# Four graph layers on one core: two layers' biases written into PSUM by ScalarE instead of added to x by GpSimd

## The chip, the core and the metric

The kernel runs on one core of a Trainium2 chip. A core has five engines with queues of their own: TensorE (PE; the loading of its weights is shown apart, as PEld), VectorE (DVE), ScalarE (ACT), GpSimd (POOL) and SyncE (SP), which here issues all DMAs. Matrix products go into PSUM, eight banks of 128 partitions x 512 fp32 elements; everything else lives in SBUF. The metric is the device time of one execution in microseconds (us), lower is better. The time before is the median of three runs, 1694.06 us (1693.2 to 1696.14).

## What is computed

32 graphs of 512 nodes with 128 features go through four residual layers, all with the same 512 x 512 adjacency of zeros and ones. Each layer normalises x over its features, takes the positive part, h, and adds the layer's result to x. In the reference, cut to what matters:

```python
# layer 0: attention-like weights from node scores
x_h = elu(h @ Wi + bi)
e = sigmoid(a_tgt[:, :, None] + a_src[:, None, :] + be[0]) * mask
recv = elu(concat([e @ x_h, x_h * sum(e)]) @ Wn + bn)
x = x + (concat([recv, x_h]) @ Wm + bm)
# layer 1: five gated steps
for _ in range(5):
    m = adj @ h; av = concat([m, m]); u3 = h @ u3_w.T + u3_b
    z, r = sigmoid(av @ w3_w.T + w3_b + u3), sigmoid(av @ w4_w.T + w4_b + u3)
    h = (1 - z) * h + z * tanh(av @ w5_w.T + w5_b + (r * h @ u5_w.T + u5_b))
x = x + h
# layer 2
x = x + (adj @ (h @ weight) + bias)
# layer 3: products with adj, adj^2, adj^3 and a weight for each
x = x + y
```

The change concerns `bm` of layer 0 and `bias` of layer 2, two vectors of 128 numbers that are the same for all nodes.

## The kernel before, in words

The kernel is written as a list of operations, which a planner orders. `op` (L55) takes an operation's engine, its assumed cost in us, a due time, the code that emits it, and the values that it reads and writes. `Plan.order` (L109) then plays the engines against each other in assumed time: each engine that is free takes the ready operation with the earliest due time, if a buffer is free for each value that it writes for the first time. What comes out is one order for each engine's queue, so any change of an operation's engine, cost or dependences makes all orders anew behind it. The planner keeps POOL's operations and DVE's operations that are marked `two` (two SBUF inputs) from overlapping in its assumed time (`shared`, L134 and L177).

A value (`Val`, L23) has a kind, and takes a buffer of that kind: "x" for a group of four graphs' x, "f" for [128, 512] SBUF tiles, "r" and "q" for rounded parts of such tiles, "s" for small statistics, "m" and "d" for DRAM scratch, and "b" for a PSUM bank. There are eight banks, and a graph's [512, 128] matrix fills one as four chunks of 128 columns (`chunks`, L277).

Graphs are staggered. The first four start 14 us apart; from then on a graph starts every 56 us and the last ones every 30, and a graph's four layers lie so far apart that layers of several graphs interleave on all engines. Layer 3 works on four graphs together, at the end of each group. What is done before the branch on the adjacency (whether it is exact in the rounded format; here it is) is ordered first; then each arm of the branch is ordered for itself, and the exact arm runs. There PE multiplies by the adjacency in rounded fp32 parts (low and high), and by weights in full fp32, which the trace shows as two records for each product.

The parts that the change touches, and that the prediction's steps name:

- `layernorm` (L448): DVE takes the moments (L457 to L460), POOL the power (L462), DVE the shift (L465), ACT four activations of one chunk each, from x to h (L470).
- `add_bias` (L436): one POOL operation for a graph that adds a broadcast [128, 128] bias tile to the graph's x in place (L437). It is called once for a graph in `first_layer` (L658, with `bm_bc`), after the layer norm has read x, and once in `layer2` (L857, with `l2b_bc`).
- `layer0` (L530): the product with Wi and an ELU (L519, L433, L522 on ACT, L524 and L526 on DVE), messages and node scores (L548, which writes two small pieces into each of two banks), the attention tiles (L599 on ACT, L602 on DVE), their sums on POOL (L621) and PE (L633, with L628 on DVE ahead of it), the products with them (L610), `own` on DVE (L636), the product with Wn, a second ELU, then the last product with the two halves of Wm into a bank `po` (L646): for each chunk two matmuls, of which the first starts the chunk anew (`start=n == 0`). `add_to_x` (L441) has DVE add the bank to x (L445).
- `layer1` (L807): products with u3T, w4T, w3T, w5T and u5T (all on L428), copies from PSUM by ACT (L417), gates on DVE (L824, L831) and ACT (L433), the new state on DVE (L841 to L845), and between steps a transpose through DVE (L369) and two DMAs, then the split into parts on ACT (L769) and DVE (L773). `times_adj` (L793) makes the adjacency products (L799).
- `layer2` (L857): parts, `times_adj`, a copy `m` from PSUM by ACT (L417), one matmul for each chunk with l2w into a bank `po` (L863), and DVE's addition to x (L445).
- `layer3` (L871): products L880 and L889 in one bank for four graphs, of which only the first starts anew; parts of it (L769, L773); DVE adds the end result to x (L901) and SP stores it (L906).

Of the kernel before, what the change touches and what calls it, by code (L numbers as in the profile page):

```python
# [28 lines left out]
        self.slot, self.writer, self.readers, self.left = None, None, [], 0  # L29


class Op:
    def __init__(self, eng, us, result, emit, two, keep):
        self.eng, self.us, self.result, self.emit, self.two, self.keep = eng, us, result, emit, two, keep
# [4 lines left out]
class Plan:  # L39
# [7 lines left out]
    def __init__(self, slots, ahead, last):  # L47
        self.ahead, self.last, self.ops, self.vals = ahead, last, [], {}
        self.free = {k: [(0.0, i) for i in range(n)] for k, n in slots.items()}
        self.until = dict.fromkeys(self.RESULT, 0.0)  # L50
        self.shared, self.now = 0.0, 0.0
        self.slack = 0.0
        self.idle = None

    def op(self, eng, us, due, emit, reads=(), writes=(), two=False, keep=0, result=None,  # L55
# [37 lines left out]
    def back_to(self, state):  # L93
# [5 lines left out]
            )  # L99
        self.free = {k: [*f] for k, f in free.items()}  # L100

    def known(self, o, to):

        own = {"PE": 0.0, "ACT": 0.13, "DVE": 0.13}
        if to.eng == o.eng in own:
            return o.known - o.result + own[o.eng]
        return o.known + (self.slack if to.eng == "PE" else 0.0)

    def order(self, end=None):  # L109

        left = [o for o in self.ops if not o.begun]
        for o in reversed(left):
            o.chain = o.us + max([0.0, *(o.result + a.chain for a in o.after)])
            if end is None:
                o.due = min(o.due, self.last - o.chain)
        by_due, oldest = sorted(left, key=lambda o: o.due), 0
        coming, ready = {e: [] for e in self.until}, {e: [] for e in self.until}
        order, events, index = [], [self.now], {}
        for i, o in enumerate(left):
            index[o] = i  # L120
            o.waits = sum(not b.begun for b in o.before)
            o.ready = max([o.earliest, *(self.known(b, o) for b in o.before if b.begun)])
            if not o.waits:
                heapq.heappush(coming[o.eng], (o.ready, i, o))
                events.append(o.ready)
        events += self.until.values()
        events += [t for f in self.free.values() for t, _ in f] + [self.shared]
        events = [max(t, self.now) for t in events]
        heapq.heapify(events)

        def begins(o, now):
            if o.due > by_due[oldest].due + self.ahead:
                return False
            if (o.two or o.eng == "POOL") and self.shared > now:  # L134
                return False
            keep = 0 if o is by_due[oldest] else o.keep
            return all(
                len(self.free[v.kind]) > keep and self.free[v.kind][keep][0] <= now
                for v in o.takes
            )  # L140

        while events:
            now = heapq.heappop(events)
            if end is not None and now >= end:
                break
            for e in self.until:
                while coming[e] and coming[e][0][0] <= now:
                    _, i, o = heapq.heappop(coming[e])
                    heapq.heappush(ready[e], (o.due, i, o))
                if self.until[e] > now:  # L150
                    continue
                passed, o = [], None
                while ready[e] and o is None:
                    x = heapq.heappop(ready[e])
                    if begins(x[2], now):
                        o = x[2]
                    else:
                        passed.append(x)
                for x in passed:
                    heapq.heappush(ready[e], x)  # L160
                if o is not None and end is not None and any(
                    c.due < o.due and t < now + 0.3 * o.us for t, _, c in coming[e]
                ):
                    heapq.heappush(ready[e], (o.due, index[o], o))
                    o = None
                if o is None and e == "PE" and end is not None and self.idle.known <= now:
                    order.append(self.idle)
                    self.until[e] = now + self.idle.us
                    heapq.heappush(events, self.until[e])
                if o is None:  # L170
                    continue
                order.append(o)
                o.begun = True
                while oldest + 1 < len(by_due) and by_due[oldest].begun:
                    oldest += 1
                o.start, self.until[e] = now, now + o.us
                if o.two or e == "POOL":  # L177
                    self.shared = self.until[e]
                for v in o.takes:
                    v.slot = self.free[v.kind].pop(0)[1]  # L180
                o.known = self.until[e] + o.result
                heapq.heappush(events, self.until[e])
                heapq.heappush(events, o.known)
                for v in o.vals:
                    v.left -= 1
                    if not v.left and v.kind:
                        self.free[v.kind].append((o.known, v.slot))
                        self.free[v.kind].sort()
                for a in o.after:
                    if a in index:  # L190
                        a.waits -= 1
                        a.ready = max(a.ready, self.known(o, a))
                        if not a.waits:
                            heapq.heappush(coming[a.eng], (a.ready, index[a], a))
        assert end is not None or len(order) == len(left), "the plan does not end: too few buffers"
        self.now = end or 0.0
        return order
# [3 lines left out]
def tile_four_graph_layers(  # L201
# [150 lines left out]
    def transposed(src, due):  # L352

        pt = Val("b")
        def emit():
            for c in range(NC):
                nc.tensor.transpose(at(pt)[:, ts(c, P)], at(src)[:, ts(c, P)], at(ident))
        op("PE", T_TR, due, emit, [src, ident], [pt])
        return pt
# [73 lines left out]
        op("ACT", us, due, lambda: nc.scalar.activation(  # L433
            at(dst), at(src), AF.Tanh, bias=at(bias), scale=scale), [src, bias], [dst])

    def add_bias(b, bias_bc, due):  # L436
        op("POOL", 1.4, due, lambda: nc.gpsimd.tensor_tensor(  # L437
            at(X[b]), at(X[b]), at(bias_bc)[:, None, :].to_broadcast([P, NC, D]), op=ALU.add),
            [X[b], bias_bc], [X[b]])

    def add_to_x(b, p, due, view=chunks, two=False):  # L441
        def add():
# [47 lines left out]
            [short, A_nat[ic]], [odd, n_odd], two=True)  # L490
    for jc in range(NC):
        pt, z = Val("b"), Val("f")
        def turn(jc=jc, pt=pt):
            for ic in range(NC):
                nc.tensor.transpose(at(pt)[:, ts(ic, P)], at(A_nat[ic])[:, ts(jc, P)], at(ident))
# [5 lines left out]
            at(mask)[:, jc, :], at(pt), 0.0, at(z), op0=ALU.is_equal, op1=ALU.add),  # L501
            [pt, z], [mask])
    p_odd = Val("b")
    def count():
        for jc in range(NC):
            nc.tensor.matmul(
# [23 lines left out]
    def layer0(b, h, due):  # L530
# [10 lines left out]
        msg, ends = Val("f"), Val("s")  # L541
        for half in range(2):
            pt = Val("b")
            def cut(pt):
                return at(pt)[:, : 2 * (P + 2)].rearrange("p (c d) -> p c d", c=2)
            def send(pt=pt, half=half):
# [41 lines left out]
                )  # L588
        if b < G:
            tgt = Val("b")  # L590
            op("PE", T_TR, d, spread, [ends, ident], [tgt])
        else:
            op("DVE", 0.1, d, turn, [ends], [flip])
# [45 lines left out]
        recv = elu(pn, bn_sb, bn_half, d + 6, 2, ALPHA / 2)  # L639

        d = due + 44
        po = Val("b")
        def emit():
            for c in range(NC):
                for n, src in enumerate((recv, xhT)):
                    nc.tensor.matmul(  # L646
                        at(po)[:, ts(c, P)], at(src)[:, ts(c, P)], at(Wm_sb)[:, n, :],
                        start=n == 0, stop=n == 1,
                    )
        op("PE", 8 * T_NARROW, d, emit, [recv, xhT, Wm_sb], [po])  # L650
        add_to_x(b, po, d)


# [3 lines left out]

    def first_layer(b):  # L658
        h = layernorm(b, begin(b))
        add_bias(b, bm_bc, begin(b))  # L660
        layer0(b, h, begin(b))

    for b in range(G):
# [22 lines left out]
    def list_rest(exact, pool):  # L686
# [10 lines left out]
        def transposed_weight(src, name, due, factor=1.0):  # L697
            cols = src.shape[1]
            t, pt, wT = Val("f"), Val("b"), const(f"{name}T", [P, P])
            load(t, src, due, 0.7, to=lambda t: t[:, :cols])  # L700
            if cols > P:
                op("DVE", 0.3, due, lambda: nc.vector.tensor_tensor(
# [43 lines left out]
        else:  # L746
# [3 lines left out]
                load(nat[ic], adj[ts(ic, P), :], 20, 1.3)  # L750
            for jc in range(NC):
                pt = Val("b")
                def turn(jc=jc, pt=pt):
                    for ic in range(NC):
                        nc.tensor.transpose(
# [99 lines left out]


        def layer2(b, h, due):  # L857
            add_bias(b, l2b_bc, due)
            m = copied(times_adj(parts(h, due, two=True), due), due)
            po = Val("b")  # L860
            def emit():
                for c in range(NC):
                    nc.tensor.matmul(  # L863
                        at(po)[:, ts(c, P)], at(m)[:, ts(c, P)], at(l2w_sb), start=True, stop=True
                    )
            op("PE", NC * T_NARROW, due + 4, emit, [m, l2w_sb], [po])
            add_to_x(b, po, due + 4)


# [106 lines left out]
```

## Time and profile before

The profile is of one execution, whose own time was 1695.31 us; its span from the first to the last instruction is 1693.5 us, at a granted TensorE clock of 0.999.

| view | what | value |
|---|---|---|
| times | median of three runs | 1694.06 us |
| times | profiled execution, and its span | 1695.31, 1693.5 us |
| groups | L428 on PE, all products with weights of layer 1 | 320 records for each of five weights, 162.3 to 164.0 us each |
| groups | L799 on PE, adjacency products | 300.2 + 151.8 us |
| groups | L889 on PE, layer 3's adjacency products | 768 records, 218.5 us, mean 421 ns |
| groups | L369 on DVE, transposes | 244, 204.3 us, mean 841 ns |
| groups | L621 on POOL, attention sums | 84, 131.4 us |
| groups | L462 on POOL, layer norm's power | 128, 155.5 us |
| groups | L445 on DVE, a bank added to x | 64, 43.2 us |

How to read it: an engine's busy share is the time in which an instruction of its own was running, as a share of the span. A group's line gives the source line, the engine, the operation, the names out<-in, shapes and count, then the busy time and the mean of one in ns, then how long the engine had been idle just before these instructions and what ended most of that. A wait's line gives who waited for whom, the sum of the waits in us, how many they were, and the longest. Matmuls are pipelined and their ends are modelled, so that a product's listed time is longer than its share of PE's time.

### The profile page before, as it was taken

To read this page: it belongs to the slowest core of one execution; us is meant where nothing else is said; L and a number is where in the kernel's file an instruction comes from. 1 tells how busy PE (TensorE), PEld (TensorE's weight loads), DVE (VectorE), ACT (ScalarE), POOL (GpSimd) and SP (SyncE) were. 2 spreads that over 40 slices of the span, in tenths; PEclk is the share of its full clock that TensorE was granted. 3 is DMA by queue.
4 is the path that set the end of the run, shared out by engine and by line. 5 is a ranking of instruction groups with operands and counts; after the bars stand their busy time and mean duration, and the time that the engine had idled before them with its cause. 6 is when DMAs were issued, how large, how long until landed. Compare 5 with 4: busy or idle time off the path is not lost.

```text
span 1693.5 us, 21347 instructions
## 1 busy us (share of the span) xinstructions
PE 1671.6 (99%) x6627; PEld 1075.1 (63%) x6627; DVE 1484.5 (88%) x3325; ACT 1100.3 (65%) x2079; POOL 381.7 (23%) x301
## 2 busy tenths in 40 slices
PE   9999999999999999999999999999999999999998
PEld 7555555556666666666666666666666666666787
DVE  6799999999999998999988899888999988878842
ACT  7766776767666666566676667666767656555540
POOL 3222202322322221222222222212222220001210
PEclk9999999999999999999999999999999999999999
DMA  3122333243333333243232333233333233222302
GB/s 94 55 76 92 96 117 92 80 127 105 100 107 100 108 93 102 73 127 92 94 100 87 100 95 112 86 114 92 113 102 94 88 100 94 78 72 88 90 5 58
DMA packets 266875, 156.57 MB, mean 92 GB/s; under 512 B 75392, under 2 KB 235008, under 8 KB 266752
## 3 DMA queue, kind: packets, MB, share of 16 engines
q1 hardware_dynamic: 266752, 155.12, 30.8%
q8 instruction: 54, 0.88, 0.2%
q14 instruction: 69, 0.57, 0.1%
HBM read 82.25 MB, written 72.81 MB: 92 GB/s over the span
## 4 chain that ended last, share of the span: by engine, by line
PE 77%; DVE 15%; ACT 4%; issue 2%; DMA 2%; SPq 0%; DVEq 0%; ACTq 0%
PE b L428 35%; PE b L799 16%; PE b L889 9%; PE b L880 5%; PE b L610 3%; PE b L646 3%; DVE f L602 2%; DVE r L773 2%; DVE f L369 2%; DVE f L824 2%; PE b L548 1%; PE b L863 1%; DVE f L841 1%; DVE f L831 1%; ACT f L470 1%
## 5 line engine op out<-in xcount | busy, mean ns | idle before, releaser
L417 ACT COPY f<-b 128x512 f32<-128x512 f32 x360 | 208.2, 586 | 168.2 <-PE b L799 114.8
L799 PE MATMUL b<-AQ,r 128*128 128x512 f32 x1024 | 300.2, 435 | 4.5 <-DVE r L773 4.5
L462 POOL TENSOR_TENSOR s<-s,nhalf 128x4 f32<-128x4 f32 x128 | 155.5, 1215 | 629.2 <-DVE s L460 610.6
L799 PEld LDWEIGHTS b<-AQ,r 128*128 128x128 f32 x1024 | 191.9, 188 | 93.1 <-issue 45.0
L824 DVE TENSOR_TENSOR f<-f,b 128x512 f32<-128x512 f32 x320 | 210.7, 673 | 30.5 <-PE b L428 23.6
L470 ACT ACTIVATE f<-x,s 128x128 f32<-128x128 f32 x512 | 210.6, 489 | 24.2 <-DVE s L465 24.0
L889 PE MATMUL b<-r,A_r 128*128 128x512 f32 x768 | 218.5, 421 | 0.0
L433 ACT ACTIVATE f<-f,b4w 128x512 f32<-128x512 f32 x160 | 115.5, 723 | 156.6 <-DVE f L824 155.7
L369 DVE STREAM_TRANSPOSE f<-f 128x512 f32<-128x512 f32 x244 | 204.3, 841 | 10.5 <-ACT f L470 10.1
L621 POOL TENSOR_TENSOR f<-f,f 128x512 f32<-128x512 f32 x84 | 131.4, 1565 | 230.1 <-DVE f L602 159.2
L428 PE MATMUL b<-f,u5T 128*128 128x512 f32 x320 | 164.0, 596 | 3.5 <-DVE f L831 3.1
L889 PEld LDWEIGHTS b<-r,A_r 128*128 128x128 f32 x768 | 139.5, 189 | 43.3 <-issue 20.1
L428 PE MATMUL b<-f,w4T 128*128 128x512 f32 x320 | 163.4, 593 | 2.5 <-ACT f L417 2.5
L428 PE MATMUL b<-f,w5T 128*128 128x512 f32 x320 | 162.9, 592 | 0.0
L428 PE MATMUL b<-f,u3T 128*128 128x512 f32 x320 | 162.6, 592 | 0.0
L428 PE MATMUL b<-f,w3T 128*128 128x512 f32 x320 | 162.3, 592 | 0.0
L773 DVE TENSOR_TENSOR r<-f,r 128x512 fp32r<-128x512 f32 x192 | 143.9, 753 | 10.8 <-ACT r L769 10.6
L799 PE MATMUL b<-A_r,r 128*128 128x512 f32 x512 | 151.8, 438 | 0.0
L880 PEld LDWEIGHTS b<-V,f 128*128 128x128 f32 x1024 | 130.9, 191 | 26.0 <-issue 20.8
L433 ACT ACTIVATE f<-b,b5w 128x512 f32<-128x512 f32 x160 | 109.3, 684 | 57.5 <-PE b L428 57.3
L433 ACT ACTIVATE f<-f,b3w 128x512 f32<-128x512 f32 x160 | 115.0, 720 | 40.0 <-DVE f L824 39.2
L841 DVE TENSOR_TENSOR f<-f,f 128x512 f32<-128x512 f32 x160 | 113.1, 709 | 29.4 <-ACT f L433 28.8
(106 smaller groups left out, 2645.5 us busy)
## 6 DMA issues: line engine op xcount, KB each, us to landing
m<-f SPq DMA_DIRECT2D x244, 256.0 KB, 2.1
f<-m SPq DMA_DIRECT2D x184, 256.0 KB, 2.9
f<-m SPq DMA_DIRECT2D x240, 64.0 KB, 2.2
x<-in_x_dram SPq DMA_DIRECT2D x32, 256.0 KB, 3.3
out_dram<-x SPq DMA_DIRECT2D x32, 256.0 KB, 2.4
f<-d SPq DMA_DIRECT2D x28, 256.0 KB, 5.4
f<-in_adj_dram SPq DMA_DIRECT2D x4, 256.0 KB, 4.1
f<-in_L_gnn_weight_dram SPq DMA_DIRECT2D x2, 224.0 KB, 3.1
```

Of the source, the lines that this page charges most:

```text
L369: op("DVE", us, due, lambda: nc.vector.transpose(view_out(at(blocks)), view_in(at(src))), [src], [blocks])
L417: op("ACT", us, due, lambda: nc.scalar.copy(at(t), at(src)), [src], [t])
L428: nc.tensor.matmul(to, at(w), of, start=start, stop=stop)
L433: op("ACT", us, due, lambda: nc.scalar.activation(at(dst), at(src), AF.Tanh, bias=at(bias), scale=scale), [src, bias], [dst])
L462: op("POOL", 1.35, due, lambda: nc.gpsimd.tensor_tensor(stat(SCALE), stat(VAR), at(neg_half), op=ALU.pow), [s, neg_half], [s])
L470: nc.scalar.activation(at(h)[:, ts(c, P)], at(X[b])[:, c, :], AF.Relu, bias=stat(SHIFT)[:, c : c + 1], scale=stat(SCALE)[:, c : c + 1],)
L621: op("POOL", 1.6, d - 10, lambda: nc.gpsimd.tensor_tensor(at(dst), at(a), at(c), op=ALU.add), [a, c], [dst])
L773: op("DVE", T_VEC, due, lambda: nc.vector.tensor_tensor(part(lo), whole(), part(hi).bitcast(F32), op=ALU.subtract), [src, hi], [lo], two=two)
L799: nc.tensor.matmul(at(pa), at(part)[:, ts(jc, P)], view(at(columns)[:, jc, :]), start=jc == n == 0, stop=jc == NC - 1 and n == PARTS - 1,)
L824: op("DVE", T_VEC, d, lambda: nc.vector.tensor_tensor(at(s), at(u), at(pg), op=ALU.add), [u, pg], [s])
L880: nc.tensor.matmul(at(pz)[:, ts(i, D)], at(hT[i])[:, ts(ic, P)], at(V[k]), start=i == 0, stop=last and i == G - 1,)
L889: nc.tensor.matmul(at(pz), at(adjT)[:, jc, ts(ic, P)], at(part), start=False, stop=jc == NC - 1 and n == PARTS - 1,)
```

## The change

`add_bias` and its 64 POOL operations go. In their place `bias_first` makes a new value of kind "b", and has ACT write the broadcast bias into that whole bank; it is planned after `own` in layer 0 and after `m` in layer 2. The last products of the two layers then take this bank as `po`, with `start=False` on every matmul, so that they add to what is there, and read it as an input for the planner.

A product with `start=False` is meant to add to what a bank holds, and the code treats a bank as fit for that only if its last user wrote it whole. The planner now notes for each bank whether its last user wrote it in pieces (`pieces`), and gives a bias only a free bank whose last user did not (`clean`). All values that are written in pieces are marked so: the transposes, L548's, `p_odd`'s, the weights' and the scores'. Elsewhere a value takes the bank that came free first, as before.

```diff
@@ Plan
+    def clean(self, now):
+        return next((n for n, (t, i) in enumerate(self.free["b"])
+                     if t <= now and not self.pieces.get(i, True)), None)
@@ order, begins
+            if any(v.added and self.clean(now) is None for v in o.takes):
+                return False
@@ order
                 for v in o.takes:
-                    v.slot = self.free[v.kind].pop(0)[1]
+                    v.slot = self.free[v.kind].pop(self.clean(now) if v.added else 0)[1]
+                    if v.kind == "b":
+                        self.pieces[v.slot] = v.pieces
@@
-    def add_bias(b, bias_bc, due):
-        op("POOL", 1.4, due, lambda: nc.gpsimd.tensor_tensor(
-            at(X[b]), at(X[b]), at(bias_bc)[:, None, :].to_broadcast([P, NC, D]), op=ALU.add),
-            [X[b], bias_bc], [X[b]])
+    def bias_first(bias_bc, after, due):
+        dst = Val("b")
+        dst.added = True
+        op("ACT", T_COPY, due, lambda: nc.scalar.copy(
+            chunks(at(dst)), at(bias_bc)[:, None, :].to_broadcast([P, NC, D])), [bias_bc, after], [dst])
+        return dst
@@ layer0
-        po = Val("b")
+        po = bias_first(bm_bc, own, d)
...
-                        start=n == 0, stop=n == 1,
+                        start=False, stop=n == 1, skip_group_check=True,
                     )
-        op("PE", 8 * T_NARROW, d, emit, [recv, xhT, Wm_sb], [po])
+        op("PE", 8 * T_NARROW, d, emit, [recv, xhT, Wm_sb, po], [po])
@@ first_layer
-        add_bias(b, bm_bc, begin(b))
@@ layer2
-            add_bias(b, l2b_bc, due)
             m = copied(times_adj(parts(h, due, two=True), due), due)
-            po = Val("b")
+            po = bias_first(l2b_bc, m, due + 4)
...
-                        at(po)[:, ts(c, P)], at(m)[:, ts(c, P)], at(l2w_sb), start=True, stop=True
+                        at(po)[:, ts(c, P)], at(m)[:, ts(c, P)], at(l2w_sb), start=False, stop=True,
+                        skip_group_check=True,
                     )
-            op("PE", NC * T_NARROW, due + 4, emit, [m, l2w_sb], [po])
+            op("PE", NC * T_NARROW, due + 4, emit, [m, l2w_sb, po], [po])
```

## The prediction

> **What bounds the kernel now.** I read, in this order: the busy shares, the stretches of the span, TensorE's (PE's) own waits, the groups of instructions that the change touches, and the timeline around two of PE's gaps.
>
> The busy shares and the costliest groups (out<-in, shapes, count | busy us, mean ns of one | idle before, and what ended it):
>
> ```profile
> PE 1671.6 (99%) x6627; PEld 1075.1 (63%) x6627; DVE 1484.5 (88%) x3325; ACT 1100.3 (65%) x2079; POOL 381.7 (23%) x301
> L417 ACT COPY f<-b 128x512 f32<-128x512 f32 x360 | 208.2, 586 | 168.2 <-PE b L799 114.8
> L769 ACT CAST r<-f 128x512 fp32r<-128x512 f32 x192 | 117.5, 618 | 16.2 <-DMA f<-m 16.0
> L437 POOL TENSOR_TENSOR x<-x,bm_bc 128x512 f32<-128x512 f32 x32 | 44.5, 1391 | 222.7 <-ACT f L470 207.1 <-DMA m<-f 13.6 <-DMA x<-in_x_dram 2.0
> L437 POOL TENSOR_TENSOR x<-x,l2b 128x512 f32<-128x512 f32 x32 | 42.8, 1337 | 151.2 <-ACT f L470 151.2
> L646 PE MATMUL b<-Wm_sb,f 128*128 128x128 f32 x512 | 62.4, 275 | 0.8 <-DVE f L526 0.8
> L863 PE MATMUL b<-l2w,f 128*128 128x128 f32 x256 | 33.7, 275 | 0.0
> ```
>
> PE is idle 1693.5 - 1671.6 = 21.9 us, and that is the whole prize: no edit on another engine can gain more. The stretches say where it lies (each engine's busy us, PE first):
>
> ```profile
> 100.00:200.00 100.00, 96.73 (x319) 53.94 (x318) 95.91 (x191) 69.67 (x128) 21.50 (x15) 1.00 0.30 91
> 200.00:300.00 100.00, 99.58 (x322) 56.57 (x321) 97.93 (x191) 67.50 (x121) 20.16 (x14) 1.00 0.33 101
> 300.00:400.00 100.00, 95.66 (x355) 58.15 (x354) 96.50 (x223) 71.25 (x140) 26.45 (x20) 1.00 0.36 103
> 400.00:1400.00 1000.00, 995.09 (x3897) 637.55 (x3896) 918.37 (x2074) 669.13 (x1265) 253.40 (x185) 1.00 0.33 99
> 1400.00:1600.00 200.00, 200.00 (x752) 127.42 (x751) 165.75 (x351) 118.81 (x216) 19.15 (x16) 1.00 0.29 86
> 1600.00:1694.00 94.00, 86.25 (x534) 76.44 (x532) 34.59 (x93) 27.51 (x58) 10.12 (x9) 0.98 0.12 36
> ```
>
> PE loses 8.0 us between 100 and 400, where VectorE (DVE) is 96 to 98% busy; 4.9 us in the thousand after that, with DVE at 92%; nothing from 1400 to 1600, with DVE at 83%; and some 7.3 us after its last product (the end of the span, with its last stores). PE starves where DVE has no room left. Its waits name the same engine:
>
> ```profile
> PE b L799 <- DVE r L773: 4.5, 3, 2.5
> PE b L428 <- DVE f L831: 3.1, 7, 0.8
> PE b L428 <- ACT f L417: 2.5, 4, 1.1
> PE b L633 <- DVE q L628: 1.3, 2, 1.0
> PE b L646 <- DVE f L526: 0.8, 1, 0.8
> PE b L610 <- DVE f L602: 0.6, 1, 0.6
> ```
>
> Of 12.8 us, DVE ends 10.3 and ScalarE (ACT) 2.5. And the timeline shows one of GpSimd's (POOL's) bias additions at work right ahead of such a gap:
>
> ```profile
> 154.94 1.71 POOL L437 TENSOR_TENSOR x<-x,bm_bc 128x512 f32<-128x512 f32 x1
> 155.45 1.75 DVE L773 TENSOR_TENSOR r<-f,r 128x512 fp32r<-128x512 f32 x1
> 157.12 0.68 DVE L841 TENSOR_TENSOR f<-f,f 128x512 f32<-128x512 f32 x1
> 157.25 0.50 PE L799 MATMUL b<-AQ,r 128*128 128x512 f32 x1 [1.36 <-DVE r L773]
> ```
>
> The L773 that PE waits for took 1.75 us beside POOL's addition; the next operation of its size, alone, 0.68.
>
> **The change, part by part.**
>
> *Removed: 64 POOL additions.* POOL gets back 44.5 + 42.8 = 87.3 us, worth nothing in itself: it stands idle 77% of the span. What counts is the stretch of DVE. I went through the trace's DVE instructions one by one and compared each with the median of its line and tiles: 43 that overlap an L437 are over 0.15 us too long, 27.2 us together (5.7 of it between 100 and 400, 15.8 between 400 and 1400), of 107.6 us of such excess in the whole kernel. The remaining POOL work (L621, L462) keeps most of the rest. How much PE gets of it no row shows. If PE's waits on a nearly full DVE go as one over DVE's idle time, then between 100 and 400 that idle time grows from 9.7 to 15.4 us and the 8.0 us shrink by 37%, 3.0 us; between 400 and 1400 it grows from 81.6 to 97.4 and the 4.9 us shrink by 16%, 0.8 us. Relief: 3.8 us. Its bounds: nothing (the next late operation, an L831 or L628, ends the same wait), and all 10.3 us that DVE ends. I take 3.8, near the share that L437 has in the excess (27.2 of 107.6, a quarter, which would be 2.6).
>
> The Trainium skill (SBUF — State Buffer, section "Who interferes with whom") says that a VectorE instruction with two SBUF inputs and a GpSimd instruction that reads SBUF exclude each other for whole instructions. The 1.75 us above agrees, but by the rule alone each of the 64 additions could cost DVE its full 1.36 us, three times the 27.2 us that the trace shows; the relief would then be 6.5 us by the same scaling (12.2 us of DVE between 100 and 400, where 9 of the 64 lie, and 54 for the 40 after), and the time 1687.8.
>
> *Added: 64 ACT copies of a broadcast [128,128] bias into a whole PSUM bank.* The trace has no ACT write to PSUM. The nearest rows of this size are 586 ns (bank to SBUF, L417) and 618 ns (SBUF to SBUF, L769): 64 x 0.6 = 38.4 us, between 36 (the shortest L417, 559 ns) and 46 (a tanh of this size, 723 ns in L433's dearest row). ACT goes from 65 to 67% of the span, in the tight stretch from 70 to about 73%. Behind such a copy in ACT's queue stand, in the changed order, mostly another L417 copy, a tanh or a cast, each 0.6 us later, and PE waits for them only where nothing else is ready. ACT's 2.5 us of ended waits grow with its smaller idle time (593 to 555 us) by 7%, 0.2 us. Nearly all copies wait for nothing but ACT's own earlier work: in the changed order of the branch that runs, 2 of 64 wait for DVE.
>
> *The products' new wait.* L646 and L863 now also need the bias in the bank. For layer 0 the copy may be planned once `own` is there; in the trace 5.5 us at least, 8 on average, lie between that L636 and the first L646, in which ACT has three activations of the ELU (2.1 us): covered. For layer 2 it follows the copy of m, and between that L417 and L863 lie 2.3 us on average, but under 0.9 us in nine graphs of 32. Cover here is the other products that the plan puts on PE in between; where it is missing the copy's 0.6 us shows. The nine bound it at 5.4 us; the lower bound is nothing. Since L863 shows 0.0 us of idle before it, I take one case, 0.5 us.
>
> *PSUM.* The bias holds a bank for those 8 and 2.3 us longer, 32 x 10.3 / 1693.5 = 0.2 banks on average. Following the banks through the trace, from the first product into one to its last reader, 3.3 of 8 are in use on average and 7 or more in under 3% of the time. Nothing. The demand for a bank whose last user wrote it whole can hold up a copy, but in each graph's course only the two small banks of L548 leave pieces after the first graphs. The product count stays (4540 rows on PE in the branch that runs, before and after), and accumulating rows exist already: L889, never started anew, takes its 421 ns with no idle time before it. Nothing.
>
> The Trainium skill (PSUM — Partial Sum Buffer, section "Summary: rules for kernel authors") speaks against this: a bank seeded by ScalarE must be seeded with zero on this chip, since ScalarE's writes leave the bank's written marks alone. No trace shows those marks; the change picks banks by their last user to meet it. It would cost correctness, not time.
>
> *The order.* The plan is made anew: PE's rows differ from the 100th of the branch on. The head is the same. At the end, three L901 (1.88 us) and three stores follow PE's last products now, in the changed order two: between 0.1 us (the adds' overlap with the last products) and 1.0 us (a store's issue). I take 0.5 off. In between, the new order lands its own gaps; with some 20 gaps of 0.3 to 2.7 us in the old one, I give them plus or minus 5 us around zero.
>
> **Sum:** -3.8 + 0.2 + 0.5 - 0.5 = -3.6 us. Against the profiled execution's own 1695.31 us (span 1693.5 and 1.8 us around it) that is 1691.7; this execution lies 1.25 us above the runs' median, 1694.06, so the forecast is 1690.5. A change below 0.2% (3.4 us: 1690.7 to 1697.4) can't be told from none.
>
> **Rivals.**
> *A hidden gain, 1693.5.* The plan already keeps POOL and two-input DVE operations apart on paper (`shared`), and most stretched DVE operations (14 of the 43 are L369, which feeds a DMA) are on no path of PE; then only the tail's 0.5 us is left. Against it: the gap at 157.25, which needs no chain of argument.
> *Slower, 1701.8: ACT takes DVE's place.* ACT takes its queue in the written order, runs at 71% from 300 to 400 and is given work where tanh (L433) already waits for DVE and is waited for in turn. If one in five of the 38.4 us shows on PE and the relief does not, that is 7.7 us on 1694.1. It decides once PE's waits on ACT rise from 2.5 to over 5.9 us with nothing gained elsewhere, or to over 10.2 with the 4.3 us of relief and tail. Against it: ACT's 35% idle time, and that 114.8 us of L417's idle time is spent waiting for PE, so PE leads there.
> *It doesn't do what it says, 1690.5:* a marked bank loses the bias, at the same time.
>
> **How the numbers follow.** Forecast 0.50 (its own range 1685 to 1694: three quarters of it below 1690.7, the rest within 0.2%), hidden 0.20 (within 0.2%), ACT 0.28 (nine tenths slower, one within), lost bias 0.02 (faster). Faster: 0.375 + 0.02 = 0.39; same: 0.125 + 0.20 + 0.03 = 0.35; slower 0.26. The range goes from 1682 (relief of all 10.3 us, and a lucky order by 2 us) to 1702 (the ACT case); the floor, without any gap of PE before its last product, lies near 1681.
>
> **What would show it.** Right: POOL near 294 us, DVE near 1457, ACT near 1139; no 1.75 us DVE rows beside anything but L621 and L462; PE's waits on DVE near 6.5 us, those on ACT under 3.5. The relief is wrong if DVE falls by 27 us and PE's idle time between 100 and 400 stays at 8. The ACT case is right if L646 or L863 wait for the copy, or L428 for L417 or L433, for over 9 us. And a new gap with none of these behind it would make the new order the cause.

## The result

The changed kernel takes 1690.22 us (median of 13 runs, 1688.85 to 1691.1) against 1694.61 us before (13 runs taken beside it, 1692.91 to 1697.71): a ratio of 0.997, 95% interval 0.9962 to 0.9979. It is faster by 4.4 us, 0.3%. The profiled execution took 1689.17 us, with a span of 1687.4.

### The profile after

Line numbers have moved: L453 is now the bias copy on ACT, L441 was L428, L820 was L799, L794 was L773, L862, L864 and L866 were L841, L843 and L845, L852 was L831, L430 was L417, L476 was L460, L619, L622, L630 and L641 were L599, L602, L610 and L621, L666 and L883 were L646 and L863, L910 was L889. First the busy shares, the groups of the new copies and of the products that add to them:

```profile
PE 1667.7 (99%) x6627; PEld 1076.8 (64%) x6627; DVE 1457.7 (86%) x3325; ACT 1127.8 (67%) x2143; POOL 295.8 (18%) x237
```

```profile
L453 ACT COPY b<-l2b 128x512 f32<-128x512 f32 x32 | 19.1, 596 | 0.0
L453 ACT COPY b<-bm_bc 128x512 f32<-128x512 f32 x32 | 19.0, 593 | 0.0
L666 PE MATMUL b<-Wm_sb,f 128*128 128x128 f32 x512 | 62.3, 275 | 0.0
L883 PE MATMUL b<-l2w,f 128*128 128x128 f32 x256 | 33.7, 275 | 0.0
```

POOL is lighter by 85.9 us and DVE by 26.8. The copies take 0.594 us each, 38.1 us together, while ACT's busy time grows by 27.4 only, because neighbouring records of ACT overlap and the busy time counts the overlap once. The products that now accumulate take the same 275 ns as before. The stretches of the span and PE's waits, as before:

```profile
100.00:200.00 100.00, 98.33 (x331) 56.54 (x330) 94.64 (x189) 70.43 (x128) 16.17 (x12) 1.00 0.30 92
200.00:300.00 100.00, 97.44 (x310) 54.90 (x309) 93.61 (x190) 65.91 (x121) 17.64 (x12) 1.00 0.29 91
300.00:400.00 100.00, 97.08 (x363) 59.42 (x362) 97.00 (x228) 76.49 (x148) 20.05 (x15) 1.00 0.39 111
400.00:1400.00 1000.00, 995.30 (x3907) 640.31 (x3906) 905.89 (x2073) 687.29 (x1311) 200.78 (x144) 1.00 0.34 99
```

```profile
PE b L441 <- DVE f L852: 6.0, 5, 1.8
PE b L441 <- ACT f L430: 2.5, 3, 1.6
PE b L820 <- DVE r L794: 1.7, 2, 1.3
PE b L441 <- DVE f L866: 1.6, 1, 1.6
...
PE b L630 <- DVE f L622: 0.6, 1, 0.6
```

These two views show far less than 6 us of gain. Between 100 and 400 PE's idle time falls from 8.0 to 7.15 us, and the waits that DVE ends from 10.3 to 9.9. PE's busy time itself fell by 3.9 us with the same 6627 records. A matmul's listed time (592 ns for 512 columns) is longer than the spacing of back-to-back ones (429 ns), so a PE that starves for a tenth of a microsecond still shows as busy. So I measured the gaps from start to start: for each matmul record, the time to the next one's start less the median that this spacing has for its group (names and shapes) in the kernel before, summed by stretch. The tail is the time from the last matmul's start to the end of the span.

| us | gaps 0 to 100 | 100 to 400 | 400 to 1400 | after 1400 | all gaps | tail | span |
|---|---|---|---|---|---|---|---|
| before | 2.5 | 11.4 | 8.3 | -1.0 | 21.3 | 7.65 | 1693.5 |
| after | 3.0 | 8.7 | 5.3 | -0.7 | 16.4 | 6.45 | 1687.4 |
| before's order, no additions | 2.3 | 9.6 | 5.5 | -1.0 | 16.5 | 7.56 | 1688.6 |
| after's order, no copies | 3.1 | 8.9 | 5.0 | -0.8 | 16.3 | 6.45 | 1687.3 |

The matmuls' own spacings sum to 1663.5 us in all four, and 1.0 us lies ahead of the first matmul. So the 6.1 us between the two profiled spans are 4.9 us of gaps and 1.2 us of tail. The last two rows are experiments; they say which part of the change made which.

### The profile page after: what moved, and what is told of

Same layout as the page of the kernel before. It is cut to its first block, busy times and chain, and to the rows that moved or that the text cites. A ratio compares the mean times of both kernels' runs of the same rounds, so it can differ in the third digit from the quotient of the medians.

```text
span 1687.4 us, 21306 instructions
## 1 busy us (share of the span) xinstructions
PE 1667.7 (99%) x6627; PEld 1076.8 (64%) x6627; DVE 1457.7 (86%) x3325; ACT 1127.8 (67%) x2143; POOL 295.8 (18%) x237
## 4 chain that ended last, share of the span: by engine, by line
PE 89%; DVE 6%; ACT 2%; DMA 1%; issue 1%; SPq 0%; DVEq 0%; ACTq 0%
PE b L441 41%; PE b L820 19%; PE b L910 10%; PE b L901 6%; PE b L630 5%; PE b L666 3%; PE b L567 2%; PE b L883 1%; PE b L300 1%; DVE f L845 1%; DVE f L622 1%; DVE r L794 1%; PE b L653 1%; ACT f L486 1%; DVE f L382 1%
## 5 line engine op out<-in xcount | busy, mean ns | idle before, releaser
L478 POOL TENSOR_TENSOR s<-s,nhalf 128x4 f32<-128x4 f32 x128 | 160.0, 1250 | 884.4 <-DVE s L476 840.9
L430 ACT COPY f<-b 128x512 f32<-128x512 f32 x360 | 208.4, 586 | 158.7 <-PE b L820 107.1
L820 PE MATMUL b<-AQ,r 128*128 128x512 f32 x1024 | 302.5, 437 | 1.3 <-DVE r L794 1.3
L820 PEld LDWEIGHTS b<-AQ,r 128*128 128x128 f32 x1024 | 192.2, 188 | 89.9 <-issue 47.4
L845 DVE TENSOR_TENSOR f<-f,b 128x512 f32<-128x512 f32 x320 | 211.6, 676 | 39.8 <-PE b L441 39.1
L382 DVE STREAM_TRANSPOSE f<-f 128x512 f32<-128x512 f32 x244 | 205.2, 844 | 21.8 <-ACT f L486 21.3
L910 PE MATMUL b<-r,A_r 128*128 128x512 f32 x768 | 222.8, 426 | 0.0
L486 ACT ACTIVATE f<-x,s 128x128 f32<-128x128 f32 x512 | 210.8, 491 | 17.3 <-DVE s L481 17.2
L641 POOL TENSOR_TENSOR f<-f,f 128x512 f32<-128x512 f32 x84 | 129.9, 1548 | 427.0 <-DVE f L622 299.0
L441 PE MATMUL b<-f,u5T 128*128 128x512 f32 x320 | 163.4, 595 | 6.0 <-DVE f L852 6.0
L910 PEld LDWEIGHTS b<-r,A_r 128*128 128x128 f32 x768 | 139.4, 189 | 46.6 <-issue 24.4
L441 PE MATMUL b<-f,w4T 128*128 128x512 f32 x320 | 163.1, 593 | 2.5 <-ACT f L430 2.5
L441 PE MATMUL b<-f,u3T 128*128 128x512 f32 x320 | 163.3, 593 | 1.7 <-DVE f L866 1.6
L441 PE MATMUL b<-f,w5T 128*128 128x512 f32 x320 | 162.5, 592 | 0.0
L441 PE MATMUL b<-f,w3T 128*128 128x512 f32 x320 | 162.1, 592 | 0.0
L820 PE MATMUL b<-A_r,r 128*128 128x512 f32 x512 | 151.1, 437 | 0.4 <-DVE r L794 0.4
L901 PEld LDWEIGHTS b<-V,f 128*128 128x128 f32 x1024 | 131.8, 191 | 26.3 <-issue 20.1
L862 DVE TENSOR_TENSOR f<-f,f 128x512 f32<-128x512 f32 x160 | 112.9, 707 | 38.0 <-ACT f L446 37.7
L794 DVE TENSOR_TENSOR r<-f,r 128x512 fp32r<-128x512 f32 x192 | 138.5, 723 | 6.4 <-ACT r L790 6.2
```

Of the source, the lines that this page charges most:

```text
L382: op("DVE", us, due, lambda: nc.vector.transpose(view_out(at(blocks)), view_in(at(src))), [src], [blocks])
L430: op("ACT", us, due, lambda: nc.scalar.copy(at(t), at(src)), [src], [t])
L441: nc.tensor.matmul(to, at(w), of, start=start, stop=stop)
L478: op("POOL", 1.35, due, lambda: nc.gpsimd.tensor_tensor(stat(SCALE), stat(VAR), at(neg_half), op=ALU.pow), [s, neg_half], [s])
L486: nc.scalar.activation(at(h)[:, ts(c, P)], at(X[b])[:, c, :], AF.Relu, bias=stat(SHIFT)[:, c : c + 1], scale=stat(SCALE)[:, c : c + 1],)
L641: op("POOL", 1.6, d - 10, lambda: nc.gpsimd.tensor_tensor(at(dst), at(a), at(c), op=ALU.add), [a, c], [dst])
```

## The experiments

Where a run is said to keep an order, PE, DVE and SP have the same rows one by one as in that kernel, and what differs is only which of POOL's or ACT's operations are issued. (The two runs with spare additions need room for their tile; there the arm of the branch that is not run gives up one constant.) Each time is a median, with the ratio to the kernel before, run beside it.

### Is it GpSimd's additions? Before's order, additions not issued

```diff
-        op("POOL", 1.4, due, lambda: nc.gpsimd.tensor_tensor(...)
+        op("POOL", 1.4, due, lambda: None,
             [X[b], bias_bc], [X[b]])
```

> The order of before on all engines, with GpSimd's 64 additions planned but not issued: x lacks the biases of layers 0 and 2. If the gain came from VectorE no longer stretched beside them (theory 1), this shows it with the order held: 27 us less of VectorE, and 3 to 5 us less of time, 1690 to 1691.5. If it came from the new order alone (theory 2), the time stays within 1 us of before, 1693.5 to 1695.

Measured: 1690.22 us against 1695.08, ratio 0.9972 (0.9961 to 0.9983). Taking the additions away, with no other row moved, gives the change's whole gain: 4.9 us, in the gaps (21.3 to 16.5 us) and not in the tail. The busy shares of this run, and the place that the prediction showed:

```profile
PE 1670.5 (99%) x6627; PEld 1077.4 (64%) x6627; DVE 1467.8 (87%) x3325; ACT 1100.5 (65%) x2079; POOL 291.8 (17%) x237
```

```profile
155.19 0.68 DVE L773 TENSOR_TENSOR r<-f,r 128x512 fp32r<-128x512 f32 x1
155.67 0.59 ACT L417 COPY f<-b 128x512 f32<-128x512 f32 x1 [0.17 <-PE b L428]
155.79 0.68 DVE L841 TENSOR_TENSOR f<-f,f 128x512 f32<-128x512 f32 x1
155.92 2.11 PE L799 MATMUL b<-AQ,r 128*128 128x512 f32 x8 [0.29 <-DVE r L773]
```

The same L773 takes 0.68 us in place of 1.75, and the same L799 waits 0.29 us in place of 1.36. DVE's busy time is 1467.8 us, 16.7 less than before, not 26.8.

TensorE's granted clock is no rival: in this profile it works against the gain. For 3.4 us it is at half (the third number from the end of the line for this stretch), which the profile of the kernel before shows nowhere between its first 5 us and its last product:

```profile
308.70:312.00 3.30, 3.30 (x9) 2.53 (x9) 3.30 (x6) 0.59 (x1) 1.10 (x1) 0.50 0.21 79
```

The same 16 products with the adjacency, in the kernel before and in this run:

```profile
309.25 3.90 PE L799 MATMUL b<-AQ,r 128*128 128x512 f32 x16 [2.50 <-DVE r L773]
```

```profile
307.28 5.50 PE L799 MATMUL b<-AQ,r 128*128 128x512 f32 x16 [2.50 <-DVE r L773]
```

So this span is 4.9 us shorter although it loses 1.6 us here. Over all executions the mean clock is 0.998, and not 0.999, about equally often in both kernels (8 of 12 before, 4 of 7 here).

### Port or queue? Before's order, additions that nobody waits for

```diff
+    aside = cpool.tile([P, 512], mybir.dt.bfloat16, tag="aside", name="aside")
...
-            at(X[b]), at(X[b]), at(bias_bc)[:, None, :].to_broadcast([P, NC, D]), op=ALU.add),
+            chunks(aside), at(X[b]), at(bias_bc)[:, None, :].to_broadcast([P, NC, D]), op=ALU.add),
```

> The order of before, GpSimd's 64 additions issued at their places, but written into a spare tile that nobody reads (as bf16, for want of room), so that they wait for no ScalarE and nobody waits for them: x lacks the biases. Theory 1 (port): the stretch of VectorE stays, and the time is that of before within 1 us. Rival (queue: the additions hold up GpSimd's queue, and the powers behind them come late): the waits are gone and the time falls by 3 us or more, to 1691 or less.

Measured: 1702.78 us, ratio 1.0047 (1.0033 to 1.006): slower by 7.7 us than with the real additions. The queue theory falls: the waits are gone and the time rose. Late powers are no cause in any case, since DVE's waits for POOL's power at L465 sum to 1.9 us in the kernel before, 2.0 without the additions and 1.9 here. Theory 1 foresaw no difference and missed what the waits did: the real additions wait for ACT's L470, and the planner keeps their planned time clear of DVE's operations marked `two`; the spare ones start at once, wherever DVE is. POOL no longer idles ahead of them (2.4 us in all, where the real additions had 374), they stretch 57 of DVE's operations by 51.6 us where the real ones stretch 29 by 21.4, and DVE is at 1508.0 us, 23.5 over before. The busy shares, and the groups of the spare additions, in this run:

```profile
PE 1675.7 (99%) x6627; PEld 1076.8 (63%) x6627; DVE 1508.0 (89%) x3325; ACT 1098.4 (65%) x2079; POOL 381.5 (22%) x301
```

```profile
L438 POOL TENSOR_TENSOR aside<-x,bm_bc 128x512 bf16<-128x512 f32 x32 | 45.2, 1412 | 2.3 <-DMA x<-in_x_dram 1.9
L438 POOL TENSOR_TENSOR aside<-x,l2b 128x512 bf16<-128x512 f32 x32 | 44.2, 1382 | 0.1
```

### What do ScalarE's copies cost? After's order, without them, and with each twice

```diff
-        op("ACT", T_COPY, due, lambda: nc.scalar.copy(...)
+        op("ACT", T_COPY, due, lambda: None,
...
-                        start=False, stop=n == 1, skip_group_check=True,
+                        start=n == 0, stop=n == 1,
```

```diff
+        def twice():
+            for _ in range(2):
+                nc.scalar.copy(chunks(at(dst)), at(bias_bc)[:, None, :].to_broadcast([P, NC, D]))
...
```

> The order of the changed kernel, with ScalarE's 64 copies planned but not issued, and the products starting each chunk anew as in before: x lacks the biases. If the copies cost what the prediction said (0.7 us), 1689.5; if ScalarE takes a real share of the gain back (theory 3), 1687 or less; if they are hidden altogether, 1690.2.

> The changed kernel and its order, with each of ScalarE's 64 copies issued twice: 38 us more on ScalarE. If ScalarE's slack hides them, as the run without copies says (0.6 us for 64), 1690.5 to 1691.5; if the first 64 used the slack up, 1693 or more.

Measured: 1689.59 us without the copies (ratio to before 0.9969, 0.9956 to 0.9981), 1690.22 with them, 1692.08 with each twice (0.9988, 0.9979 to 0.9997). The first 64 cost about 0.6 us, which is less than the intervals tell apart; the next 64 cost 1.9 us by the medians (about 3 by the ratios to the kernel before, each with its own runs beside it), over what was expected. Almost nothing waits for the copies; the view of L453 in the changed kernel says who does:

```profile
L453 ACT COPY b<-bm_bc x32: 573/587/670, 38.8 to 1394.3; 128x512 f32<-128x512 f32 x32
L453 ACT COPY b<-l2b x32: 578/596/617, 298.1 to 1617.6; 128x512 f32<-128x512 f32 x32
...
who waited for it (us, times):
  PEld b L883: 0.5, 2
```

The columns are the shortest, median and longest in ns, and the first and last start. Two products of layer 2 wait 0.5 us in all; with the copies doubled six of them wait 3.3 us. ACT's slack is there, but it is not endless.

### The additions put back into after's order

```diff
     def layernorm(b, due, beside=None):
...
+            if beside is not None:
+                nc.gpsimd.tensor_tensor(
+                    chunks(aside), at(X[b]), at(ones)[:, None, :].to_broadcast([P, NC, D]), op=ALU.add)
...
```

> The changed kernel and its order, with 64 GpSimd additions of the same size put back behind the layer norms, into a spare bf16 tile that nobody reads. Theory 1: VectorE is stretched again by 20 to 35 us, and the time goes back by 3 to 5 us, to 1693 to 1695. Theory 2 (order alone): it stays within 1 us of 1690.2.

Measured: 1707.44 us, ratio 1.007 (1.0056 to 1.0083): 17.2 us over the changed kernel, far more than the 3 to 5 expected. DVE goes from 1457.7 to 1500.7 us, 43 us more, and the gaps from 16.4 to 34.7:

```profile
PE 1674.7 (98%) x6627; PEld 1075.4 (63%) x6627; DVE 1500.7 (88%) x3325; ACT 1128.4 (66%) x2143; POOL 382.4 (22%) x301
```

The direction is theory 1's. The size was wrong for two reasons: these additions, too, run where no plan put them, so that DVE is stretched by 43 us and not by 20 to 35; and each microsecond of stretch cost more than was assumed. The real additions cost 4.9 us of time for 16.7 us of DVE, the spare ones in before's order 12.6 us for 40.2 (both against the run without additions), and these 17.2 for 43: 0.29, 0.31 and 0.40 us for each. Whether the last is higher because DVE is fuller or because of the other order, these runs can't tell.

### What is a new order worth? The same kernels with one planner number changed

```diff
-        op("POOL", 1.4, due, lambda: nc.gpsimd.tensor_tensor(
+        op("POOL", 1.36, due, lambda: nc.gpsimd.tensor_tensor(
```

That is the kernel before; and the changed one:

```diff
-        op("ACT", T_COPY, due, lambda: nc.scalar.copy(
+        op("ACT", 0.59, due, lambda: nc.scalar.copy(
```

> The kernel before with one number changed: the planner is told 1.36 us for GpSimd's addition in place of 1.4, which makes PE's order new from the 125th row of the branch. Nothing else changes, so the difference to before is what a new order alone is worth. If orders scatter by the 5 us that the prediction allowed, a difference of 2 to 7 us either way is likely; if PE's gaps come from VectorE's load and hardly from the order, it stays within 1.5 us of 1694.8.

> The changed kernel with one number changed: the planner is told 0.59 us (what the copies took) for ScalarE's copy in place of 0.5. Another order of the same work: within 1.5 us of 1690.2 if the order is worth little, 2 to 7 us away if the gain of the change was an order's luck.

> The order of the run with 1.36 us told for the addition (which took 1701.7 us), with GpSimd's 64 additions planned but not issued: x lacks the biases. If that order lost its 7.4 us because the additions fell on worse places, it comes to within 1.5 us of 1690.2, as the order of before does without them. If the loss is the order's own, the time falls by the additions' 3 to 6 us only, to 1695.5 to 1699.

Measured: 1701.68 us for before's new order (ratio 1.0043, 1.0029 to 1.0056), 7.4 us slower for a number that changes no work. After's new order: 1690.06 (0.9974, 0.9964 to 0.9984), the same as the changed kernel. And before's new order without the additions: 1696.14 (1.0008, 0.9999 to 1.0017). Put side by side:

| median us | with the additions | without | the additions cost |
|---|---|---|---|
| before's order | 1695.08 | 1690.22 | 4.9 |
| the order for 1.36 us | 1701.68 | 1696.14 | 5.5 |
| the order itself costs | 6.6 | 5.9 | |

(The 7.4 us are against the runs of before beside that kernel, the 6.6 against those of the first experiments.) The two effects are separate. The additions cost about 5 us in either order, and the other order is worse by about 6 with or without them. The half clock is a part of these figures: the profile of the other order has 6.8 us of it after its longest gap, which cost 2.7 us, and without additions 3.4 us, which cost 1.6. With that taken off the profiled spans, the additions cost 6.5 and 6.2 us and the order 5.5 and 5.8. The changed kernel's order, measured without its copies (1689.59), stands 0.6 us from before's order without its additions (1690.22): between these two orders there is next to nothing. The shorter tail (1.1 us) and the half clock (no execution of the first has a mean clock under 0.999, four of seven of the second have) would account for more than that, and two medians can't tell it apart.

### Planner costs as the trace has them

```diff
-    T_VEC, T_COPY, T_ACT, T_DMA = 0.61, 0.5, 0.6, 0.45
+    T_VEC, T_COPY, T_ACT, T_DMA = 0.68, 0.59, 0.7, 0.45
```

> The changed kernel with the planner told what the operations took in the trace: VectorE's 512 columns 0.68 us in place of 0.61, ScalarE's copies 0.59 in place of 0.5 and its activations 0.7 in place of 0.6. If PE's gaps come from plans that drift from the chip, this beats the changed kernel by 2 to 8 us, 1682 to 1688. If the plan then leaves gaps of its own because it sees VectorE full, it is slower by 2 to 10 us.

Measured: 1695.82 us (1.001, 1.0001 to 1.0019), 5.6 us slower than the changed kernel. Its gaps are 14.8 us between 100 and 400 (1.7 of them at half clock), where the changed kernel has 8.7, and 2.6 between 400 and 1400, where it has 5.3. Truer costs gave a better plan for the long middle and a worse one for the crowded start. With one order of each this can't be told from an order's luck.

### The next two-input work on GpSimd: the attention sums

In the changed kernel the POOL operations that still stretch DVE are the sums of the attention tiles (L641). First with two of the three additions of each sum not issued, in after's order:

```diff
-            def add(dst, a, c):
-                op("POOL", 1.6, d - 10, lambda: nc.gpsimd.tensor_tensor(
+            def add(dst, a, c, issue=False):
+                op("POOL", 1.6, d - 10, lambda: issue and nc.gpsimd.tensor_tensor(
                     at(dst), at(a), at(c), op=ALU.add), [a, c], [dst])
-            add(sums[0], es[0], es[1])
+            add(sums[0], es[0], es[1], True)
             add(sums[1], es[2], es[3])
             add(sums[0], sums[0], sums[1])
```

> The changed kernel and its order, with only the first of the three GpSimd additions of each attention sum issued (28 of 84 left; the row sums of layer 0 are then of two of the four tiles). If GpSimd's two-input additions cost VectorE by the port wherever they stand, VectorE loses most of the 48.7 us by which these stretch it, and the time falls by 4 to 8 us, to 1682 to 1686. If only the bias additions stood in a bad place, it stays within 1.5 us of 1690.2.

Measured: 1678.55 us, ratio 0.9904 (0.9889 to 0.9919), 11.7 us under the changed kernel; DVE 1436.6 us, 21.1 less; gaps 5.9 us in all. The time fell by more than theory 1 expected (4 to 8 us), although DVE's excess (the time by which operations beside one of POOL's exceed the median of their own form) fell only from 48.9 to 26.3 us, and theory 1 had most of it gone. The time is also under the 1681 us that the prediction called a floor. Part of the gain may be that the sums themselves are ready sooner, which this run can't separate.

Of the 26 DVE operations that the remaining 28 additions stretch, 23 are L622, which makes the tiles: the first sum starts as soon as two tiles are there, while DVE makes the third. So the additions were exchanged, with nothing left out:

```diff
-            def add(dst, a, c):
+            def add(dst, a, c, after=()):
...
-            add(sums[0], es[0], es[1])
-            add(sums[1], es[2], es[3])
+            add(sums[0], es[2], es[3])
+            add(sums[1], es[0], es[1], [es[3]])
             add(sums[0], sums[0], sums[1])
```

> The changed kernel with the attention sums' first two additions exchanged: e2 + e3 first, then e0 + e1, then their sum, so that GpSimd starts only when VectorE has made all four tiles. Nothing is left out; the plan is made anew. Theory 1 says that the 22 or so L602 operations that the first sum stretches by a microsecond each are spared: VectorE's stretch falls from 48.7 us to under 35, and at 0.2 to 0.5 us of time for each of its microseconds the kernel gains 3 to 7 us, to 1683 to 1687, with the new order's own luck of up to 6 us either way on top. If the stretch only moves to other operations, it stays near 1690.

> The same exchange with the planner also told 0.59 us for the bias copy: a second order of the same work, to tell the exchange from an order's luck. Theory 1: stretch under 35 us again, and a mean of the two of 1683 to 1687.

Measured: 1687.11 us (0.9954, 0.9941 to 0.9968) and 1688.23 us (0.9956, 0.9942 to 0.9969). L622 in the changed kernel and in the first of these two:

```profile
L622 DVE SCALAR_TENSOR_TENSOR f<-f,mask 128x512 f32<-128x512 f32 x128 | 106.2, 883 | 4.5 <-ACT f L619 4.4
```

```profile
L622 DVE SCALAR_TENSOR_TENSOR f<-f,mask 128x512 f32<-128x512 f32 x128 | 81.2, 691 | 6.8 <-ACT f L619 6.8
```

No L622 is stretched any more, and DVE's excess falls from 48.9 to 32.6 and 33.7 us, as expected. The 24.6 us of L622 are gone, and 8 to 10 us have come back on other operations, 3 of it on L476 (1.6 us, now 4.7 and 4.2). The gain over the changed kernel is 2 to 3 us, at the low end of what was expected for the first and short of it for the second; the mean of the two, 1687.7, lies just outside the expected 1683 to 1687. Against the kernel before it is 0.45%; the intervals of these two ratios overlap that of the changed kernel (0.9962 to 0.9979), so the step beyond it is likely and not sure. Given that one planner number moved an order by 7 us, two orders that agree are support, and no proof, that the exchange itself is the cause.

## Why the prediction was right, point by point

**The time and the sign** were right: 1690.5 forecast, 1690.22 measured. Against the kernel before, -3.6 us was forecast and -4.4 measured; the two times lie closer because the kernel before itself came out 0.55 us higher beside it. Not every term behind the sum was right.

**What bounds the kernel** was right: PE's gaps are the prize, and with PE's rows held, less stretch of DVE makes them smaller and more makes them larger. The view was wrong. The 21.9 us of idle time and the waits' lines are only those gaps that outlast a matmul's listed time; what I had foreseen for them (waits on DVE near 6.5 us) did not come, 9.9 us stayed, although the gain did come. The sign that I named for a wrong relief (DVE down by 27 us and PE's idle time between 100 and 400 still at 8) nearly came too: 26.8 and 7.15. The start-to-start gaps carry the gain. The floor near 1681 came from the same view, and the run with fewer sums, at 1678.55, went below it.

**The relief** was forecast at 3.8 us, 3.0 between 100 and 400 and 0.8 between 400 and 1400. With the order held it is 4.9 us in time, and in the gaps 1.8 us in the first stretch and 2.8 in the second. The 1.8 holds the 1.6 us lost at half clock; without it the first stretch gave 3.4. So the sum was low, and the step that failed is the scaling by one over DVE's idle time in the long middle: at 92% of DVE it gave 2.8 us in place of 0.8. That the sum came near is partly luck, for its input was too large (next point).

**The stretch of DVE** was mis-sized. I gave the additions 43 stretched operations and 27.2 us. 14 of the 43 are L369, DVE's transposes, which has two forms: 160 that read contiguous rows, with a median of 0.701 us, and 84 that read in a 128 x 4 pattern, 1.1 us. I compared with the median over both, so that the slower form counted as stretched. Compared form by form, 29 operations and 21.4 us remain, and DVE's busy time fell by 16.7 us when the additions alone went. The changed kernel's 26.8 us agree with my 27 by chance: its other order also has the sums stretch DVE by 48.7 us in place of 56.7. The rival of the hidden gain leaned on the same 14 operations.

**The rule on exclusive ports** of the Trainium skill (SBUF — State Buffer, "Who interferes with whom") would have given 6.5 us of relief (6.4 by the numbers beside it) if each addition cost its full length; 4.9 was measured, between that and my 3.8. The trace agrees with the rule's kind: what is stretched reads two SBUF tensors, or is the small L460. The full length for each of 64 was my upper bound and far off: additions of 1.36 us took 16.7 us from DVE, not 87. With the additions freed of their waits the excess was 51.6 us in place of 21.4, so where the additions stood was worth more than half of it.

**The copies** were put at 0.7 us (0.2 and 0.5) and measured at about 0.6; their length at 0.6 us, measured 0.594. ACT's busy time was put near 1139 us and is 1127.8. The rival in which ACT takes DVE's place did not come, since PE's waits on ACT stayed at 2.5 us.

**The tail** was put at -0.5 us and is -1.2 in the profile, beyond the 1.0 that I gave as its bound. **The order** was given plus or minus 5 us around zero. Zero was right here; the 7.4 us of another order show that the width was rather too small, and that the forecast was good partly by luck.

**The banks and the marks** cost nothing that shows: the 768 accumulating records take 275 ns as before, and only 0.5 us of PE's waits lead to a copy. The rival of the lost bias did not come: the sums hold the biases. The marks themselves are seen in no trace here.

## What to carry to other kernels

When a kernel is 99% busy on TensorE, look at the spacing of matmul starts and not at busy time or waits: gaps shorter than a matmul's listed time are in neither, and here they held most of the gain. An operation off the critical path can still cost time by stretching the operations of an engine that is nearly full; take it away with the order held to see its price, since a new order from the planner moved the time here by anything from nothing to 7 us. Before calling an instruction stretched, compare it with its own access pattern.

## What the runs showed of the hardware that I had not expected

GpSimd's small powers (L462, 128x4, 1.2 us each) stretch nothing of DVE. In the kernel before, 133 of DVE's large operations with two SBUF inputs run beside a power and no other operation of POOL, 38 of them wholly within its listed time, and none is over its median by more than 0.013 us. GpSimd's 128x512 additions, hardly longer (1.36 to 1.57 us on average), stretch by a microsecond: up to 1.1 us on operations of 0.68. How long an instruction of GpSimd shows in the profile does not say how long it keeps DVE out.

Among DVE's operations, those with a PSUM input (L824, L445, L773 from a bank), the moments (L457, L459) and the transposes (L369) are not stretched beside the bias additions, however often they overlap (0.03 us over their median at most). L460, with 128x4 elements and one tensor input, is stretched in all 10 cases, from 0.17 us to 0.81 on average:

```profile
302.69 1.28 POOL L437 TENSOR_TENSOR x<-x,l2b 128x512 f32<-128x512 f32 x1
...
303.42 0.59 DVE L460 TENSOR_SCALAR s<-s 128x4 f32<-128x4 f32 x1
...
305.09 0.17 DVE L460 TENSOR_SCALAR s<-s 128x4 f32<-128x4 f32 x1
```

This is the timeline of the kernel before: the first L460 runs beside an addition, the second does not.

A gap of PE can cost twice. In seven of the fourteen profiles the granted clock falls to half for 3.4 or 6.8 us in the middle of the run, and each time this begins within 5 us of the start of a gap of 2.0 to 4.8 us; the products in it lost 1.4 to 2.7 us. The gap alone does not decide it: the kernel before has one of 2.7 us at the same products as the run without additions, and its clock stays up.
